# Seven-product spreading with sums left in PSUM, and a planner that picks each operation's engine first

## The chip, the cores and the metric

The kernel runs on one NeuronCore of a Trainium2 chip. The metric is the time on the device in microseconds; the time before is the median of three runs. The profile is of one further execution, whose span is 1522.8 us at a granted TensorE clock of 0.999.

The engines are named as in the profile: PE is TensorE's matmuls, PEld its weight loads, DVE is VectorE, ACT is ScalarE, POOL is GpSimd (called Pool here), SP issues the transfers.

## What is computed

64 graphs of 256 nodes with 128 features (`x`, 64 x 256 x 128, float32) pass through four layers that share one 256 x 256 adjacency matrix. Each layer is a residual with a layer norm: `x = norm(x + layer(x))`. The first layer is the one that the change touches most:

```python
def step(h, _):                       # 5 times
    m_in = jnp.einsum('nm,bmd->bnd', in_matrix, h)     # in_matrix = out_matrix = adj
    m_out = jnp.einsum('nm,bmd->bnd', out_matrix, h)
    av = jnp.concatenate([m_in, m_out], axis=-1)
    u3 = h @ u3_w.T + u3_b
    z = jax.nn.sigmoid(av @ w3_w.T + w3_b + u3)
    r = jax.nn.sigmoid(av @ w4_w.T + w4_b + u3)
    hv = jnp.tanh(av @ w5_w.T + w5_b + (r * h @ u5_w.T + u5_b))
    return (1.0 - z) * h + z * hv
```

The second layer mixes two linear maps of the nodes by a softmax of the edges, the third is an attention over the neighbours followed by a small perceptron, the fourth sums seven weighted propagations up to `adj^3`.

## The kernel before

**Tiles.** Two graphs make a pair; there are 32 pairs. A pair's state is one tile of 128 partitions x 512 columns, four blocks of 128 x 128: two graphs by two halves of the nodes.

**Layer 0.** In each of five steps the state `h` (nodes on partitions) is multiplied by the adjacency matrix ("spread", giving `mT` with features on partitions), and the gates follow: products L679, L680, L687, L694 and L695 of 512 columns, three tanh on ACT (L683, L689, L697), four elementwise operations on DVE (L685, L699, L700, L702). The new state is transposed by `turn` (L520 to L528), either by a DVE block transpose and two transfers over HBM, or by four TensorE transposes (L514). `BY_DMA` says for each place how many of the last pairs use TensorE.

**Spreading.** `spread` (L539) makes the two graphs' 256 x 256 product from four matmuls of 256 columns. `spread7` (L562) makes the same from seven matmuls of 128 columns (the Strassen-Winograd scheme). Four small sums of blocks of `h` come first, L573 to L576 (recorded at L558), on DVE or Pool. The products land in the four 128-column parts of one PSUM bank: X, Y, Z, V. Two of the parts are used again for a later product after they have been read. The results are put together outside PSUM by two copies (L569 on ACT, L570 on DVE) and four additions `plus` on DVE (L566): three of 128 columns and one of 256. `FIRST` and `FINAL` say how many pairs at either end use the plain spread: none at the start, the last three.

**The planner.** Nothing runs in the order of the text. Each operation is recorded in `Schedule.add` with its possible engines and a time for each, and `Schedule.order` is a list scheduler: in each turn it takes, of all operations whose inputs are ready and for which a tile is free, the one with the least key. Its result is the fixed order of every engine's queue; on the chip the engines run their queues in that order and wait for each other by semaphores. What the planner assumes:

- A dependent operation on another engine sees a result `LAG` plus a part by engine (`SEEN`) after its end. All times but TensorE's are multiplied by `MARGIN`.
- `USES`: a DVE operation with two SBUF inputs (DVE+) and every Pool operation hold a common resource PORT, so that the plan never has two of them at once.
- Where an operation may run on several engines, every way is a candidate of its own, and its key is its end (with `SPARE` of the engine); an operation with one way has its start as the key. After that comes how late the pair is against its due time (`DUE`, `LAST_DUE` for the `LAST` last pairs, `HOLD` by layer).
- `CLASSES` is the number of tiles of each kind. PS are the eight PSUM banks.

In `stats` and `scale_stats` each normalization has two small Pool operations: adding epsilon (L604, L648, L650) and a power of -0.5 (L607, L651), both on 128 x 4.

Of the kernel before, what the change touches and what calls it, by code (L numbers as in the profile page):

```python
# [9 lines left out]
ALU = mybir.AluOpType  # L10
AX = mybir.AxisListType

P = 128
N = 256
D = 128
STEPS = 5

BY_DMA = {"h": 0, "y": 2, "x1": 3, "x2": 2, "w": 3, "z": 1, "x3": 2}

WARM = 4  # L20


FAST = (0, 1, 2, 3, 4)
FIRST, FINAL = 0, 3

TURN, TT = 0.44, 0.61
LN_EPS = 1e-5
# [9 lines left out]
ROWS = ["l1_bias", "bp", "b1", "gat_g", "gat_b", "b2"]  # L37


CLASSES = {"X": (512, 15), "T": (512, 3), "A": (512, 34), "H": (520, 4), "B": (1024, 6), "S": (32, 64), "PS": (512, 8), "D": (512, 4), "E": (1024, 8)}  # L40

SEEN = {"PE": 0.23, "ACT": 0.16, "DVE": 0.16, "POOL": 0.12, "SP": 0.0}

USES = {"DVE+": ("DVE", "PORT"), "POOL": ("POOL", "PORT")}

AGAIN = {"DVE": 0.12, "POOL": 0.12}

SPARE = {"DVE": 0.0, "DVE+": 0.0, "POOL": 0.0}


DUE, LAST_DUE, LAST = 20.0, 9.0, 8

MARGIN, LAG = 1.03, 0.8

HOLD = (0.0, -20.0, 0.0, 80.0)


def mm(cols):
# [35 lines left out]
class Op:  # L94
    def __init__(self, pair, ways, reads, writes, number, dma):
        self.pair, self.ways, self.reads, self.writes, self.number, self.dma = pair, ways, reads, writes, number, dma
        self.seen = LAG + (sum(dma) if dma else SEEN[ways[0][0].rstrip("+")])
        self.before, self.then, self.waits, self.ready, self.rest = {}, [], 0, 0.0, 0.0


class Schedule:
# [29 lines left out]
    def order(self, tiles):  # L131
        for op in self.ops:
            op.waits = len(op.before)
            for b in op.before:
                b.then.append(op)
            for v in op.holds:
                v.left += 1
        for op in reversed(self.ops):
            us = min(w[1] for w in op.ways) + op.seen
            op.rest = us + max((x.rest for x in op.then if x.pair == op.pair), default=0.0)  # L140
        free = {cls: [(0.0, t) for t in ts] for cls, ts in tiles.items()}
        full = {}
        engines = dict.fromkeys([*SEEN, "PORT"], 0.0)
        ready = [op for op in self.ops if not op.waits]
        out, moved = [], 0.0
        while ready:
            best = None
            for op in ready:
                held = 0.0
                for v in op.holds:  # L150
                    if v.cls and v.ap is None:
                        held = max(held, min((t for t, a in free[v.cls] if full.get(id(a)) or not v.seeded), default=1e9))
                if held == 1e9:
                    continue
                for engine, us, fn in op.ways:
                    us = us if engine == "PE" else us * MARGIN
                    start = max(op.ready, held, *(engines[e] for e in USES.get(engine, (engine,))))
                    late = self.due(op.pair) - op.rest + HOLD[op.layer] if op.pair >= 0 else -1e4
                    key = (start + (us + SPARE.get(engine, 0.0) if len(op.ways) > 1 else 0.0), late, op.number)
                    if best is None or key < best[0]:  # L160
                        best = key, start, op, engine, us, fn
            if best is None:
                raise RuntimeError("no operation can start: too few tiles")
            _, start, op, engine, us, fn = best
            ready.remove(op)
            for v in op.holds:
                if v.cls and v.ap is None:
                    slot = min((s for s in free[v.cls] if full.get(id(s[1])) or not v.seeded), key=lambda s: s[0])
                    free[v.cls].remove(slot)
                    v.ap = slot[1]  # L170
            end = start + us
            engines.update(dict.fromkeys(USES.get(engine, (engine,)), end))
            if op.dma:
                wait, move, seen = op.dma
                moved = max(moved, end + wait) + move * MARGIN
                op.seen = moved + seen - end + LAG
            out.append((start, op.number, op, fn))
            for v in op.holds:
                v.left -= 1
                v.end = max(v.end, end + op.seen)  # L180
                if not v.left and v.cls:
                    free[v.cls].append((v.end, v.ap))
                    full[id(v.ap)] = v.full or v.seeded
            for x in op.then:
                x.waits -= 1
                same = engine != "SP" and x.ways[0][0].rstrip("+") == engine.rstrip("+")
                x.ready = max(x.ready, end + (AGAIN.get(engine.rstrip("+"), 0.0) if same else op.seen))
                if not x.waits:
                    ready.append(x)

            op.tiles = {v: v.ap for v in op.holds}
        assert len(out) == len(self.ops), "operations that wait for one another"
        self.span = max(engines.values())
        return [(op, fn) for _, _, op, fn in sorted(out, key=lambda x: x[:2])]
# [3 lines left out]
def kernel(ctx: ExitStack, tc: tile.TileContext, x, xT, adj, adjT, mats, cols, rows, out):  # L198
# [17 lines left out]
    def dve(us, fn, r, w):  # L216
        S.add([("DVE", us, fn)], r, w)
# [2 lines left out]
        S.add([("DVE+", us, fn)], r, w)  # L220

    def pool(us, fn, r, w):
        S.add([("POOL", us, fn)], r, w)

    def dve_or_pool(fn, r, w):

# [234 lines left out]

    aTt = fixed([4, P], "aTt")
    blk_a = lambda j, i: aT.ap[:, j, i * P:(i + 1) * P]
    for k, (p_, q_) in enumerate(((lambda: blk_a(0, 1), lambda: blk_a(0, 0)), (lambda: blk_a(1, 1), lambda: aTt.ap[:, 0, :]),
                                  (lambda: blk_a(1, 1), lambda: blk_a(0, 1)), (lambda: blk_a(1, 0), lambda: aTt.ap[:, 1, :]))):
        dve(0.25, lambda k=k, p_=p_, q_=q_: nc.vector.tensor_sub(aTt.ap[:, k, :], p_(), q_()), [aT, aTt], [aTt])
    centre(vx, lambda: vx.ap, 2)
    centre(vq, lambda: vq.ap, 2)

# [74 lines left out]
    def spread7(h, right, terms):  # L544


        sv, t, o = Value("A", name="sums"), bank(), Value("A", name="mT")
        p1, p2, p3, p4 = (Part(sv) for _ in range(4))
        X, Y, Z, V = (Part(t) for _ in range(4))
        o1, o2, o3 = (Part(o) for _ in range(3))  # L550
        blk = lambda v, k, n=1: v.at(512)[:, k * P:(k + n) * P]
        H = lambda b, j: lambda: blk(h, 2 * b + j)
        B = lambda j, i: lambda: right.ap[:, j, i * P:(i + 1) * P]
        T = lambda k: lambda: terms.ap[:, k, :]
        s1, s2, s3, s4 = (lambda k=k: blk(sv, k) for k in range(4))

        def add(o, x, y, op, r, w):
            fn = lambda e: e.tensor_tensor(o(), x(), y(), op=op)  # L558
            S.add([("DVE+", 0.2, lambda: fn(nc.vector)), ("POOL", 0.42, lambda: fn(nc.gpsimd))], r, w)

        def product(k, left, rt, r, w, start=False):
            pe(mm(128), lambda: nc.tensor.matmul(blk(t, k), left(), rt(), start=start, stop=True, skip_group_check=True),  # L562
               [*r, right, terms], w)

        def plus(to, k, other, r, w, n=1):
            dve(0.065 + 0.135 * n, lambda: nc.vector.tensor_add(to(), t.at(4, P)[:, k:k + n, :], other()), r, w)  # L566

        def copy(to, k, r, w):
            S.add([("ACT", 0.18, lambda: nc.scalar.copy(to(), blk(t, k))),  # L569
                   ("DVE", 0.2, lambda: nc.vector.tensor_copy(to(), blk(t, k)))], r, w)  # L570
        product(0, H(0, 0), B(0, 0), [h], [X, Y, Z, V], start=True)
        copy(lambda: blk(o, 3), 0, [X], [o3])
        add(s1, H(1, 0), H(1, 1), ALU.add, [h], [p1])  # L573
        add(s2, s1, H(0, 0), ALU.subtract, [h, p1], [p2])
        add(s3, H(0, 0), H(1, 0), ALU.subtract, [h], [p3])
        add(s4, H(0, 1), s2, ALU.subtract, [h, p2], [p4])  # L576
        product(0, H(0, 1), B(1, 0), [h, X], [X])
        copy(lambda: blk(o, 0), 0, [X], [o])
        product(1, s2, T(1), [p2, Y], [Y])
        plus(lambda: blk(sv, 1), 1, lambda: blk(o, 3), [Y, o3], [p2])  # L580
        product(2, s1, T(0), [p1, V], [V])
        product(3, s3, T(2), [p3, Z], [Z])
        plus(lambda: blk(sv, 0), 2, lambda: blk(sv, 1), [V, p2], [p1])
        product(2, s4, B(1, 1), [p4, V], [V])
        plus(lambda: blk(o, 3), 3, lambda: blk(sv, 0), [Z, p1, o3], [o])
        product(3, H(1, 1), T(3), [h, Z], [Z])
        plus(lambda: o.at(4, P)[:, 1:3, :], 2, lambda: blk(sv, 1)[:, None, :].to_broadcast([P, 2, P]), [V, Z, p2], [o], 2)
        return o

    def stats(y, eps=None):  # L590
# [306 lines left out]
```

## Time and profile before

| | |
|---|---|
| time, median of 3 runs | 1525.11 us (1524.67 to 1527.51) |
| span of the profiled execution | 1522.8 us |
| L562: products of seven, 2030 matmul records | 128 columns each |
| L539: plain spreads | 888 records of 256 columns |
| L679, L680, L687, L694, L695: gates | 320 records each, 512 columns |
| L566: additions out of PSUM | 435 of 128 columns, 145 of 256 |
| L569 and L570: copies out of PSUM | 265 on ACT, 25 on DVE |
| small sums of spread7 (L558) | 271 on DVE, 309 on Pool |
| L651 and L607: power on Pool, 128 x 4 | 192, median 1.04 us |

A float32 matmul stands in the records as two matmul instructions and two weight loads. In a line of the profile come the line of the kernel, engine, operation, `out<-in` by the program's names, the shapes and the count, then the busy time and the mean of one in nanoseconds; the idle time of that engine ahead of such instructions follows with what ended it. In a line of waits stand who waited, after `<-` for whom, the sum in us, the number of times and the longest. In a timeline line stand the start and the length in us, and in square brackets the idle time before it.

### The profile page before, as it was taken

How to read it: one execution, taken by the hardware profiler on the slowest of the kernel's cores; microseconds unless marked ns; L12 is line 12 of the kernel's file. 1: busy time of each engine (PE TensorE's matmuls, PEld its weight loads, DVE VectorE, ACT ScalarE, POOL GpSimd, SP SyncE). 2: the span in 40 equal slices, each digit the busy share in tenths (PEclk: the TensorE clock that was granted, in tenths of full speed). 3: DMA queues.
4: the chain of work that ended last, by engine and by line, in shares of the span. 5: the costliest groups of instructions: out<-in, count | busy, mean ns of one | idle time of the engine just before them, and what ended most of it. 6: DMA issues, size and time to landing. Idle time of an engine off the chain costs nothing.

```text
span 1522.8 us, 26241 instructions
## 1 busy us (share of the span) xinstructions
PE 1502.2 (99%) x7190; PEld 1063.2 (70%) x7190; DVE 1296.3 (85%) x3443; ACT 936.2 (61%) x2805; POOL 562.4 (37%) x784
## 2 busy tenths in 40 slices
PE   9999999999999999999999999999999999999998
PEld 6565656666666677677666776766767666788997
DVE  8988888888989898888998888899888788889763
ACT  2444445666776666656757567677657566768763
POOL 4322223243435433433443344334434132245542
PEclk9999999999999999999999999999999999999999
DMA  7544456576868788686696796767975877776441
GB/s 220 113 97 82 93 117 125 125 159 122 170 132 164 155 169 171 136 164 137 140 177 128 162 185 138 152 134 173 167 147 128 169 133 153 149 149 139 106 89 49
DMA packets 933874, 213.86 MB, mean 140 GB/s; under 512 B 715616, under 2 KB 929248, under 8 KB 933728
## 3 DMA queue, kind: packets, MB, share of 16 engines
q1 hardware_dynamic: 933728, 212.19, 68.6%
q8 instruction: 58, 0.95, 0.3%
q14 instruction: 88, 0.72, 0.2%
HBM read 115.55 MB, written 96.53 MB: 139 GB/s over the span
## 4 chain that ended last, share of the span: by engine, by line
PE 90%; DVE 6%; issue 1%; SPq 1%; DMA 1%; ACT 0%; POOL 0%; POOLq 0%; DVEq 0%; ACTq 0%
PE ps L562 14%; PE ps L539 12%; PE ps L694 8%; PE ps L695 8%; PE ps L687 8%; PE ps L679 8%; PE ps L680 8%; PE ps L716 7%; PE ps L786 4%; PE ps L830 3%; PE ps L822 3%; PE ps L823 3%; PE ps L746 2%; DVE a L566 1%; SPq L528 1%
## 5 line engine op out<-in xcount | busy, mean ns | idle before, releaser
L566 DVE TENSOR_TENSOR a<-ps,a 128x128 f32<-128x128 f32 (+1 forms) x580 | 174.5, 313 | 89.8 <-PE ps L562 75.4
L562 PEld LDWEIGHTS ps<-aTt,a 128*128 128x128 f32 x1102 | 160.9, 192 | 60.1 <-issue 42.4
L683 ACT ACTIVATE a<-ps,bzrh 128x512 f32<-128x512 f32 x160 | 109.8, 686 | 138.3 <-PE ps L680 118.2
L697 ACT ACTIVATE a<-ps,bzrh 128x512 f32<-128x512 f32 x160 | 109.9, 687 | 130.3 <-PE ps L695 126.4
L562 PE MATMUL ps<-aTt,a 128*128 128x128 f32 x1102 | 180.0, 278 | 4.8 <-ACT a L569 3.7
L558 POOL TENSOR_TENSOR a<-a 128x128 f32<-128x128 f32 x138 | 81.8, 606 | 236.2 <-DMA a<-e 112.1
L694 PE MATMUL ps<-a,w 128*128 128x512 f32 x320 | 163.8, 594 | 0.2 <-DVE h L748 0.2
L695 PE MATMUL ps<-a,u5h 128*128 128x512 f32 x320 | 163.5, 592 | 0.2 <-DVE a L685 0.2
L680 PE MATMUL ps<-a,w 128*128 128x512 f32 x320 | 163.4, 592 | 0.0
L687 PE MATMUL ps<-a,w 128*128 128x512 f32 x320 | 162.5, 593 | 0.0
L520 DVE STREAM_TRANSPOSE a<-a 128x512 f32<-128x512 f32 x218 | 152.0, 700 | 3.1 <-ACT a L662 0.4
L562 PEld LDWEIGHTS ps<-aT,a 128*128 128x128 f32 x754 | 118.2, 191 | 52.1 <-issue 34.9
L689 ACT ACTIVATE a<-ps,bzrh 128x512 f32<-128x512 f32 x160 | 109.7, 687 | 68.1 <-PE ps L687 61.5
L716 PEld LDWEIGHTS ps<-W,a 128*128 128x128 f32 x1024 | 131.0, 192 | 26.1 <-issue 22.2
L569 ACT COPY a<-ps 128x128 f32<-128x128 f32 x265 | 66.3, 266 | 129.7 <-PE ps L562 81.1
L562 PE MATMUL ps<-aT,a 128*128 128x128 f32 x754 | 136.7, 278 | 5.5 <-DVE a L566 3.4
L651 POOL TENSOR_TENSOR s<-s,neg_half 128x4 f32<-128x4 f32 x128 | 136.9, 1070 | 9.9
L716 PE MATMUL ps<-W,a 128*128 128x128 f32 x1024 | 136.5, 275 | 0.1
L679 PE MATMUL ps<-a,W 128*128 128x512 f32 x256 | 130.9, 593 | 0.0
L231 ACT COPY a<-ps 128x512 f32<-128x512 f32 (+1 forms) x162 | 82.6, 513 | 73.8 <-PE ps L539 36.7
L643 ACT ACTIVATE a<-ps 128x128 f32<-128x128 f32 x428 | 112.5, 282 | 23.1 <-PE ps L716 8.6
L648 POOL TENSOR_SCALAR s<-s 128x4 f32<-128x4 f32 x96 | 29.0, 302 | 249.2 <-ACT a L643 218.9
(197 smaller groups left out, 3302.2 us busy)
## 6 DMA issues: line engine op xcount, KB each, us to landing
e<-a SPq DMA_DIRECT2D x278, 256.0 KB
a<-e SPq DMA_DIRECT2D x1112, 64.0 KB
e<-b SPq DMA_DIRECT2D x29, 512.0 KB
b<-e SPq DMA_DIRECT2D x116, 128.0 KB
x<-x_in SPq DMA_DIRECT2D x32, 256.0 KB
t<-xT_in SPq DMA_DIRECT2D x32, 256.0 KB
a<-d SPq DMA_DIRECT2D x32, 256.0 KB
y_out<-a SPq DMA_DIRECT2D x32, 256.0 KB
```

Of the source, the lines that this page charges most:

```text
L520: dve(n / 512 * 0.55 + 0.09, lambda: nc.vector.transpose(st.at(n), i.at(n)), [i], [st])
L539: nc.tensor.matmul(t.at(2, N)[:, b, :], tokens(i)[:, 2 * b + j, :], right.ap[:, j, :], start=(b == j == 0), stop=(j == 1), skip_group_chec ...
L562: pe(mm(128), lambda: nc.tensor.matmul(blk(t, k), left(), rt(), start=start, stop=True, skip_group_check=True), [*r, right, terms], w)
L566: dve(0.065 + 0.135 * n, lambda: nc.vector.tensor_add(to(), t.at(4, P)[:, k:k + n, :], other()), r, w)
L643: nc.scalar.activation(tokens(junk)[:, c, :], v.at(len(tiles), D)[:, k, :], AF.Square, scale=D ** -0.5, accum_out=mv()[:, c, 1:2])
L651: pool(1.02, lambda: nc.gpsimd.tensor_tensor(rs(), rs(), neg_half.ap, op=ALU.pow), [s, neg_half], [s])
L679: nc.tensor.matmul(t.at(512), mat("u3"), hT.at(512), start=True, stop=False)
L680: nc.tensor.matmul(t.at(512), w4.ap, mT.at(512), start=False, stop=True)
L687: pe(mm(512), lambda t=t, mT=mT: nc.tensor.matmul(t.at(512), w3.ap, mT.at(512), start=False, stop=True, skip_group_check=True), [w3, mT, t ...
L694: nc.tensor.matmul(t.at(512), w5.ap, mT.at(512), start=True, stop=False)
L695: nc.tensor.matmul(t.at(512), u5h.ap, r.at(512), start=False, stop=True)
L716: nc.tensor.matmul(tokens(t)[:, c, :], tokens(i)[:, c, :], w(), start=(first and k == c == 0), stop=(k == len(lefts) - 1), skip_group_chec ...
```

## The change

It does three things, and sets the planner's constants anew.

1. `spread7` uses a Winograd form in which the sums need PSUM as the accumulator: four products in turn are added onto part X, which is read after each; two onto V; one stands in Y. Copies (now four, on ACT or DVE) take X and V into the result's blocks, and three additions of 128 columns on DVE add further parts. Two of the four small sums become one operation of 256 columns. The terms of the adjacency matrix (`aTt`) change sign to match.
2. Pool's operations with one way (`pool`, the small operations of the normalizations) become POOL-, which takes the Pool engine but not PORT.
3. `Schedule.order` first chooses each operation's engine by its end with `SPARE`, and then compares operations by the start on that engine.

```diff
-BY_DMA = {"h": 0, "y": 2, "x1": 3, "x2": 2, "w": 3, "z": 1, "x3": 2}
+BY_DMA = {"h": 1, "y": 0, "x1": 3, "x2": 3, "w": 0, "z": 4, "x3": 0}
-FIRST, FINAL = 0, 3
+FIRST, FINAL = 2, 0
-CLASSES = {"X": (512, 15), "T": (512, 3), "A": (512, 34), "H": (520, 4), "B": (1024, 6), ...}
+CLASSES = {"X": (512, 15), "T": (512, 4), "A": (512, 30), "H": (520, 6), "B": (1024, 5), ...}
-USES = {"DVE+": ("DVE", "PORT"), "POOL": ("POOL", "PORT")}
+USES = {"DVE+": ("DVE", "PORT"), "POOL": ("POOL", "PORT"), "POOL-": ("POOL",)}
-SPARE = {"DVE": 0.0, "DVE+": 0.0, "POOL": 0.0}
+SPARE = {"DVE": 0.6, "DVE+": 0.0, "POOL": -0.3}
-DUE, LAST_DUE, LAST = 20.0, 9.0, 8
+DUE, LAST_DUE, LAST = 15.0, 12.0, 12
-MARGIN, LAG = 1.03, 0.8
+MARGIN, LAG = 1.1, 0.3
-HOLD = (0.0, -20.0, 0.0, 80.0)
+HOLD = (0.0, -20.0, 0.0, 40.0)
...
+                way = None
                 for engine, us, fn in op.ways:
                     us = us if engine == "PE" else us * MARGIN
                     start = max(op.ready, held, *(engines[e] for e in USES.get(engine, (engine,))))
-                    late = self.due(op.pair) - op.rest + HOLD[op.layer] if op.pair >= 0 else -1e4
-                    key = (start + (us + SPARE.get(engine, 0.0) if len(op.ways) > 1 else 0.0), late, op.number)
-                    if best is None or key < best[0]:
-                        best = key, start, op, engine, us, fn
+                    end = start + us + SPARE.get(engine, 0.0)
+                    if way is None or end < way[0]:
+                        way = end, start, op, engine, us, fn
+                late = self.due(op.pair) - op.rest + HOLD[op.layer] if op.pair >= 0 else -1e4
+                key = (way[1], late, op.number)
+                if best is None or key < best[0]:
+                    best = key, *way[1:]
...
     def pool(us, fn, r, w):
-        S.add([("POOL", us, fn)], r, w)
+        S.add([("POOL-", us, fn)], r, w)
...
-        product(0, H(0, 0), B(0, 0), [h], [X, Y, Z, V], start=True)
-        copy(lambda: blk(o, 3), 0, [X], [o3])
-        add(s1, H(1, 0), H(1, 1), ALU.add, [h], [p1])
-        add(s2, s1, H(0, 0), ALU.subtract, [h, p1], [p2])
-        add(s3, H(0, 0), H(1, 0), ALU.subtract, [h], [p3])
-        add(s4, H(0, 1), s2, ALU.subtract, [h, p2], [p4])
-        product(0, H(0, 1), B(1, 0), [h, X], [X])
-        copy(lambda: blk(o, 0), 0, [X], [o])
-        product(1, s2, T(1), [p2, Y], [Y])
-        plus(lambda: blk(sv, 1), 1, lambda: blk(o, 3), [Y, o3], [p2])
-        product(2, s1, T(0), [p1, V], [V])
-        product(3, s3, T(2), [p3, Z], [Z])
-        plus(lambda: blk(sv, 0), 2, lambda: blk(sv, 1), [V, p2], [p1])
-        product(2, s4, B(1, 1), [p4, V], [V])
-        plus(lambda: blk(o, 3), 3, lambda: blk(sv, 0), [Z, p1, o3], [o])
-        product(3, H(1, 1), T(3), [h, Z], [Z])
-        plus(lambda: o.at(4, P)[:, 1:3, :], 2, lambda: blk(sv, 1)[:, None, :].to_broadcast([P, 2, P]), [V, Z, p2], [o], 2)
+        product(0, H(0, 0), B(0, 0), [h], [X, Y, V], start=True)
+        sum_(0.335, 0.8, lambda e: e.tensor_sub(sv.at(4, P)[:, 0:2], h.at(4, P)[:, 0::2], h.at(4, P)[:, 2:4]), [h], [p1])
+        sum_(0.2, 0.46, lambda e: e.tensor_sub(s2(), s1(), H(0, 0)()), [h, p1], [p2])
+        sum_(0.2, 0.46, lambda e: e.tensor_add(s4(), s2(), H(0, 1)()), [h, p2], [p4])
+        copy(0, 0, [X], [o0])
+        product(1, s1, T(0), [p1, V], [V])
+        copy(3, 1, [V], [o3])
+        product(2, H(0, 1), B(1, 0), [h, Y], [Y])
+        plus(0, 2, [Y, o0], [o, o0])
+        product(0, s2, T(1), [p2, X], [X])
+        copy(1, 0, [X], [o1])
+        product(1, s4, B(1, 1), [p4, V], [V])
+        plus(1, 1, [V, o1], [o, o1])
+        product(0, s3, T(2), [p1, X], [X])
+        plus(3, 0, [X, o3], [o, o3])
+        product(0, H(1, 1), T(3), [h, X], [X])
+        copy(2, 0, [X], [o])
```

More of the change, by code (lines that the diff above doesn't have):

```diff
@@ L37 @@
 ROWS = ["l1_bias", "bp", "b1", "gat_g", "gat_b", "b2"]
-CLASSES = {"X": (512, 15), "T": (512, 3), "A": (512, 34), "H": (520, 4), "B": (1024, 6), "S": (32, 64), "PS": (512, 8), "D": (512, 4), "E": (1024, 8)}
+CLASSES = {"X": (512, 15), "T": (512, 4), "A": (512, 30), "H": (520, 6), "B": (1024, 5), "S": (32, 64), "PS": (512, 8), "D": (512, 4), "E": (1024, 8)}
 SEEN = {"PE": 0.23, "ACT": 0.16, "DVE": 0.16, "POOL": 0.12, "SP": 0.0}
-USES = {"DVE+": ("DVE", "PORT"), "POOL": ("POOL", "PORT")}
+USES = {"DVE+": ("DVE", "PORT"), "POOL": ("POOL", "PORT"), "POOL-": ("POOL",)}
 AGAIN = {"DVE": 0.12, "POOL": 0.12}
-SPARE = {"DVE": 0.0, "DVE+": 0.0, "POOL": 0.0}
-DUE, LAST_DUE, LAST = 20.0, 9.0, 8
-MARGIN, LAG = 1.03, 0.8
-HOLD = (0.0, -20.0, 0.0, 80.0)
+SPARE = {"DVE": 0.6, "DVE+": 0.0, "POOL": -0.3}
+DUE, LAST_DUE, LAST = 15.0, 12.0, 12
+MARGIN, LAG = 1.1, 0.3
+HOLD = (0.0, -20.0, 0.0, 40.0)
 def mm(cols):
@@ L96, in __init__ @@
         self.pair, self.ways, self.reads, self.writes, self.number, self.dma = pair, ways, reads, writes, number, dma
-        self.seen = LAG + (sum(dma) if dma else SEEN[ways[0][0].rstrip("+")])
+        self.seen = LAG + (sum(dma) if dma else SEEN[ways[0][0].rstrip("+-")])
         self.before, self.then, self.waits, self.ready, self.rest = {}, [], 0, 0.0, 0.0
@@ L185, in order @@
                 x.waits -= 1
-                same = engine != "SP" and x.ways[0][0].rstrip("+") == engine.rstrip("+")
-                x.ready = max(x.ready, end + (AGAIN.get(engine.rstrip("+"), 0.0) if same else op.seen))
+                same = engine != "SP" and x.ways[0][0].rstrip("+-") == engine.rstrip("+-")
+                x.ready = max(x.ready, end + (AGAIN.get(engine.rstrip("+-"), 0.0) if same else op.seen))
                 if not x.waits:
@@ L463 @@
     blk_a = lambda j, i: aT.ap[:, j, i * P:(i + 1) * P]
-    for k, (p_, q_) in enumerate(((lambda: blk_a(0, 1), lambda: blk_a(0, 0)), (lambda: blk_a(1, 1), lambda: aTt.ap[:, 0, :]),
-                                  (lambda: blk_a(1, 1), lambda: blk_a(0, 1)), (lambda: blk_a(1, 0), lambda: aTt.ap[:, 1, :]))):
-        dve(0.25, lambda k=k, p_=p_, q_=q_: nc.vector.tensor_sub(aTt.ap[:, k, :], p_(), q_()), [aT, aTt], [aTt])
+    dve(0.25, lambda: nc.vector.tensor_sub(aTt.ap[:, 0, :], blk_a(0, 1), blk_a(0, 0)), [aT], [aTt])
+    for k, other in ((1, lambda: aTt.ap[:, 0, :]), (2, lambda: blk_a(0, 1))):
+        dve(0.25, lambda k=k, other=other: nc.vector.scalar_tensor_tensor(aTt.ap[:, k, :], blk_a(1, 1), -1.0, other(),
+                                                                         op0=ALU.mult, op1=ALU.subtract), [aT, aTt], [aTt])
+    dve(0.25, lambda: nc.vector.tensor_add(aTt.ap[:, 3, :], aTt.ap[:, 1, :], blk_a(1, 0)), [aT, aTt], [aTt])
     centre(vx, lambda: vx.ap, 2)
@@ L544, in spread7 @@
     def spread7(h, right, terms):
[L547 to L550, printed above, removed]
+        sv, t, o = Value("A", name="sums"), Value("PS", name="ps"), Value("A", name="mT")
+        p1, p2, p4 = (Part(sv) for _ in range(3))
+        X, Y, V = (Part(t) for _ in range(3))
+        o0, o1, o3 = (Part(o) for _ in range(3))
         blk = lambda v, k, n=1: v.at(512)[:, k * P:(k + n) * P]
@@ L554, in spread7 @@
         T = lambda k: lambda: terms.ap[:, k, :]
[L555 to L559, printed above, removed]
+        s3, s1, s2, s4 = (lambda k=k: blk(sv, k) for k in range(4))
         def product(k, left, rt, r, w, start=False):
@@ L563, in product, with sum_ @@
                [*r, right, terms], w)
-        def plus(to, k, other, r, w, n=1):
-            dve(0.065 + 0.135 * n, lambda: nc.vector.tensor_add(to(), t.at(4, P)[:, k:k + n, :], other()), r, w)
+        def sum_(us, us_pool, fn, r, w):
+            S.add([("DVE+", us, lambda: fn(nc.vector)), ("POOL", us_pool, lambda: fn(nc.gpsimd))], r, w)
         def copy(to, k, r, w):
-            S.add([("ACT", 0.18, lambda: nc.scalar.copy(to(), blk(t, k))),
-                   ("DVE", 0.2, lambda: nc.vector.tensor_copy(to(), blk(t, k)))], r, w)
@@ L581, in spread7 @@
-        product(2, s1, T(0), [p1, V], [V])
-        product(3, s3, T(2), [p3, Z], [Z])
-        plus(lambda: blk(sv, 0), 2, lambda: blk(sv, 1), [V, p2], [p1])
-        product(2, s4, B(1, 1), [p4, V], [V])
-        plus(lambda: blk(o, 3), 3, lambda: blk(sv, 0), [Z, p1, o3], [o])
-        product(3, H(1, 1), T(3), [h, Z], [Z])
-        plus(lambda: o.at(4, P)[:, 1:3, :], 2, lambda: blk(sv, 1)[:, None, :].to_broadcast([P, 2, P]), [V, Z, p2], [o], 2)
+            S.add([("ACT", 0.18, lambda: nc.scalar.copy(blk(o, to), blk(t, k))),
+                   ("DVE", 0.2, lambda: nc.vector.tensor_copy(blk(o, to), blk(t, k)))], r, w)
@@ new lines, in plus @@
+        def plus(to, k, r, w):
+            dve(0.2, lambda: nc.vector.tensor_add(blk(o, to), blk(t, k), blk(o, to)), r, w)
+        product(0, H(0, 0), B(0, 0), [h], [X, Y, V], start=True)
[3 more added lines that the diff above has]
+        copy(0, 0, [X], [o0])
```

## The prediction

> **What bounds the kernel now.** I read the page's engine totals first, then the stretches (busy time of each engine by window), then who waited for whom on TensorE, then the chain of waits, and last the timeline around single TensorE waits. Page, part 1:
>
> ```profile
> span 1522.8 us, 26241 instructions
> PE 1502.2 (99%) x7190; PEld 1063.2 (70%) x7190; DVE 1296.3 (85%) x3443; ACT 936.2 (61%) x2805; POOL 562.4 (37%) x784
> ```
>
> TensorE is idle for only 1522.8 - 1502.2 = 20.6 us, so the kernel can win no more than idle time, the last few microseconds, and columns that it no longer streams. Where the idle time lies (columns: window, its length, then busy us of PE, PEld, DVE, ACT, POOL):
>
> ```profile
> 0.00:25.00 25.00, 22.08 (x90) 15.52 (x91) 20.56 (x68) 6.18 (x14) 11.09 (x27) 1.00 0.98 281
> 25.00:50.00 25.00, 24.25 (x127) 16.24 (x126) 24.96 (x67) 9.62 (x23) 15.41 (x25) 1.00 0.42 95
> 50.00:200.00 150.00, 150.00 (x599) 87.57 (x598) 126.17 (x296) 62.52 (x126) 33.01 (x56) 1.00 0.47 99
> 200.00:600.00 400.00, 394.15 (x1877) 267.63 (x1876) 353.57 (x930) 254.90 (x753) 152.27 (x211) 1.00 0.74 146
> 600.00:1100.00 500.00, 495.46 (x2443) 353.03 (x2443) 444.36 (x1178) 331.29 (x1036) 200.04 (x263) 1.00 0.77 154
> 1100.00:1500.00 400.00, 399.64 (x1984) 309.27 (x1983) 320.20 (x877) 265.49 (x842) 146.82 (x199) 1.00 0.66 133
> 1500.00:1523.00 23.00, 16.60 (x80) 13.97 (x78) 6.48 (x31) 6.17 (x17) 3.78 (x6) 0.92 0.16 46
> ```
>
> Idle: 3.7 us in the first 50, none to 200, 10.4 us from 200 to 1100 (there VectorE is 88 to 89% busy), 0.4 us to 1500, and 6.4 us at the end, after the last product. Who ended TensorE's waits between 50 and 1500 us:
>
> ```profile
> PE ps L562 <- DVE a L566: 4.4, 11, 1.1
> PE ps L562 <- ACT a L569: 3.3, 9, 0.5
> PE ps L786 <- ACT a L697: 0.7, 1, 0.7
> PE ps L562 <- DVE a L570: 0.6, 2, 0.4
> ```
>
> Nearly all stand before a product of spread7 (L562), waiting for an addition (L566) or copy (L569, L570) out of its own PSUM bank. A matmul's end is modelled, and hides part of a wait: summing each matmul's start-to-start distance beyond the median of its form, I get 26.8 us lost, 6.1 of it in the first 50 us and 20.7 later. The timeline shows what makes an addition late:
>
> ```profile
> 730.29 1.45 POOL L733 TENSOR_TENSOR a<-x,rbc 128x512 f32<-128x512 f32 x1
> 730.54 1.48 DVE L761 CUSTOM_DVE_ANT_0 b<-a,maskb 128x256 f32<-128x256 f32 x1
> 731.70 1.44 POOL L777 TENSOR_TENSOR b<-b,a 128x512 f32<-128x512 f32 x1
> 731.95 1.47 DVE L761 CUSTOM_DVE_ANT_0 b<-a,maskb 128x256 f32<-128x256 f32 x1
> 733.36 1.49 DVE L566 TENSOR_TENSOR a<-ps,a 128x128 f32<-128x128 f32 x6
> 734.80 0.46 PE L562 MATMUL ps<-aT,a 128*128 128x128 f32 x2 [0.84 <-DVE a L566]
> ```
>
> L761's median is 0.417 us; twice in a row it takes about 1.5 while Pool works on a large tile, six additions pile up behind it, and TensorE waits. Over the trace 163 VectorE instructions are more than 60 ns over the median of their form, 65 us in all, each beside a Pool operation of 128 columns or more.
>
> [...] Here one record of 512 columns starts 429 ns before the next, 256 takes 216 and 128 takes 112[...]; a product is two records. [...] the 71 VectorE instructions that ran beside the small power operations alone (L648, L651) together lost 0.03 us[...]. [...] Here 128 columns take 0.201 us start to start, 256 take 0.334. [...]
>
> **The change, part by part.** Counts are those of the two built programs, their instructions standing in the order that the planner gives.
>
> *TensorE's columns.* A plain spread is eight records of 256 columns, 8 x 0.216 = 1.73 us; the seven products are 14 x 0.112 = 1.57. FIRST 2 and FINAL 0 make 150 spreads of seven in place of 145: 5 x 0.16 = -0.8 us. BY_DMA leaves 56 transposes on TensorE in place of 64, each 0.109: -0.9. Together -1.7 us, and that is certain.
>
> *VectorE.* Before, 145 double additions (0.334) and 435 single ones (0.201) emptied the bank: 48.4 + 87.4 = 135.8 us. After, 450 single ones: 90.5. The four small sums before each spread become one of double width and two single: on VectorE 271 x 0.202 = 54.7 becomes 86 x 0.334 + 42 x 0.202 = 37.2. Copies out of the bank go 25 to 32, +1.4. Against it the choice of engines moves 144 pieces of the layer norm from ScalarE to VectorE (L615, 0.338 long, about 0.26 apart): +37. Fewer evacuations, scalings and statistics on VectorE give -30, more multiplications and additions of constants +11. Sum: about -43 us of 1296, so 82% in place of 85%.
>
> *ScalarE.* Copies 265 to 568 at 0.161: +49; the layer norm's pieces 232 to 88 at 0.385: -55; scaling, evacuation and squares +20. About +14, 62%. It has room.
>
> *Pool.* 309 single sums at 0.458 become 64 double and 258 single: with the planner's 0.8 for the double (none is in the trace) about 169 us against 142; eight large operations fewer, -10. [...] the collisions stay.
>
> *The round trips.* This is the part that can go either way. In the new spread7 one PSUM quarter is used four times: product, copy, product, copy, product, addition, product, copy. The shortest round trip product, copy, product in the trace is some 0.52 us, with an addition 0.55. I counted the TensorE work that stands, in each program's order, between a product and the next one that needs its quarter emptied. Before, the median is 5.2 us for the copied quarter, one trip in ten below 2.4. After, the medians of the four trips are 2.4 to 3.1 us, one in ten below 1.5 to 1.8, none below 0.88. The planner's LAG of 0.3 in place of 0.8 does that. So at one trip in ten the cushion is about 1 us, and a single collision costs the same: a lone one mostly fits, two in a row don't. In return only one of the four trips goes through VectorE. Before, the sixth product waited for two chained additions and the seventh for a third, each in VectorE's queue behind L761 or L699. MARGIN 1.1 (1.03 before) plans VectorE, ScalarE and Pool slower than they are, which gives back cushion at every queue. Leaving the small power operations off the port removes 192 x (1.02 + 0.23) = 240 us of holding[...].
>
> *Start.* Before, the first products wait for sums, copies and additions on a VectorE that also builds the constants: about 2.2 us in two gaps at 8.7 and 11.9 us. After, pairs 0 and 1 use plain spreads, which need the input alone, and the gate products of pair 0 follow after the second spread, behind which the evacuation of the first hides: -2 us. [...]
>
> *End.* The last product, statistics, power, scaling and output stay a chain of 6 us; two squares on ScalarE in place of VectorE's statistics are worth -0.2 at most. I count 0.
>
> *BY_DMA, DUE, LAST, HOLD, CLASSES.* They reorder pairs. Transfers ended a single TensorE wait of 0.4 us (L746); I cost them at nothing, with the DMA's lag in the range.
>
> Sum: -1.7 columns, -2 start, and of the 20.7 us lost in the middle I take half, because two of the three VectorE steps that release products are gone while the cushion halves: -10. 1525.1 - 13.7 = about 1511.5 us.
>
> **The rivals.**
> *Nearly all waits go.* For it: after 1100 us TensorE already runs 399.64 of 400 with VectorE at 80%, and VectorE now falls by 3 points. Against: the late stretch has few spreads of seven (148 of 2030 records). Losing all but 3 us of the middle gives 1525.1 - 1.7 - 2 - 17.7 = about 1503.7.
> *No change.* The shorter distances lose as much again as the lighter VectorE saves, and 10 to 14 us come back: 1523. For it: the waits today come although distances are twice as long.
> *Slower.* VectorE is late by 65 / 163 = 0.4 us on average at 163 instructions; the changed program has about 400 round trips closer than 2.2 us where before had 29. If 60 of those meet a collision and lose 0.25 us each, +15 on top of today's, with the -3.7 that is safe: about 1536. Against: three of the four trips go through ScalarE[...].
>
> **How the numbers follow.** Forecast 0.50, nearly all waits go 0.18, no change 0.12, slower 0.20. Faster is the first two: 0.68. The range runs from 1502 (all waits gone and a little off the end) to 1533, above which I leave half of the slower case.
>
> **What would show it.** Right: TensorE busy 99.5% with its idle time before 1500 us at 7 or less; VectorE near 1253 us; first gap at 8.7 us gone. Wrong: more waits of products for copies on ScalarE (the cushion was too small), waits for DMA at the sums, or VectorE not falling since collisions grow with the double sums on Pool.

## The result and the profile after

The changed kernel took 1516.24 us (median of 4 runs, 1516.03 to 1516.94) against 1525.13 us (1524.67 to 1527.51) before, a ratio of 0.9939 with an interval of [0.9922, 0.9957]. The span of the profiled execution went from 1522.8 to 1514.4 us. The engine totals on the page of the kernel after:

```profile
span 1514.4 us, 26315 instructions
PE 1499.2 (99%) x7212; PEld 1059.6 (70%) x7212; DVE 1219.7 (81%) x3240; ACT 960.5 (63%) x3056; POOL 587.0 (39%) x789
```

VectorE lost 76.6 us of work, ScalarE gained 24.3, Pool 24.6, and TensorE is idle for 15.2 us where it was 20.6. The same stretches as before the change (window, its length, busy us of PE, PEld, DVE, ACT, POOL):

```profile
0.00:25.00 25.00, 23.29 (x91) 16.36 (x92) 14.26 (x46) 8.36 (x18) 6.01 (x13) 1.00 1.02 291
25.00:50.00 25.00, 25.00 (x97) 15.02 (x97) 23.75 (x55) 12.13 (x28) 17.12 (x27) 1.00 0.49 117
50.00:200.00 150.00, 148.42 (x575) 88.20 (x574) 110.46 (x236) 70.01 (x163) 31.30 (x48) 1.00 0.47 97
200.00:600.00 400.00, 396.93 (x1903) 269.02 (x1902) 343.80 (x886) 266.81 (x828) 160.28 (x207) 1.00 0.76 153
600.00:1100.00 500.00, 497.88 (x2428) 353.34 (x2427) 410.44 (x1102) 320.26 (x1038) 203.01 (x270) 1.00 0.73 149
1100.00:1500.00 400.00, 399.25 (x2089) 310.97 (x2088) 316.13 (x919) 277.84 (x961) 166.72 (x220) 1.00 0.68 135
1500.00:1514.50 14.50, 8.38 (x38) 6.72 (x36) 0.85 (x2) 5.08 (x23) 2.52 (x4) 0.92 0.24 61
```

The first 50 us lose 1.7 us of TensorE in place of 3.7, and 200 to 1100 us lose 5.2 in place of 10.4; but 50 to 200 us, which lost nothing, now lose 1.6. Who ended TensorE's waits between 50 and 1500 us, after the change:

```profile
PE ps L565 <- DVE a L576: 4.1, 10, 0.5
PE ps L565 <- ACT a L572: 1.8, 5, 0.4
```

Both the products that waited for additions (L566 before, L576 now) and those that waited for copies on ScalarE (L569 before, L572 now) did so for less time; no DMA is left among them. Measured as in the prediction (start-to-start distances of matmuls beyond the median of their form), TensorE lost:

| us lost | first 50 | 50 to 1500 | after 1500 | sum |
|---|---|---|---|---|
| before | 6.0 | 20.5 | 0.3 | 26.8 |
| after | 2.25 | 17.7 | 0.3 | 20.2 |

So the 8.4 us of the spans are 3.8 from the start, 2.8 from the middle, and 1.8 from columns that are no longer streamed and the rounding of the rest. The middle, for which most was expected, gave the least for its size.

### The profile page after: what moved, and what is told of

Read it like the earlier page. It is cut to its first block, busy times and chain, and to the rows that moved or that the text cites. A ratio compares the mean times of both kernels' runs of the same rounds, so it can differ in the third digit from the quotient of the medians.

```text
span 1514.4 us, 26315 instructions
## 1 busy us (share of the span) xinstructions
PE 1499.2 (99%) x7212; PEld 1059.6 (70%) x7212; DVE 1219.7 (81%) x3240; ACT 960.5 (63%) x3056; POOL 587.0 (39%) x789
## 4 chain that ended last, share of the span: by engine, by line
PE 96%; DVE 1%; DMA 1%; ACT 1%; issue 0%; POOL 0%; SPq 0%; POOLq 0%; ACTq 0%; DVEq 0%
PE ps L565 16%; PE ps L545 12%; PE ps L701 9%; PE ps L702 9%; PE ps L686 9%; PE ps L687 9%; PE ps L694 9%; PE ps L723 7%; PE ps L793 4%; PE ps L829 3%; PE ps L830 3%; PE ps L837 3%; PE ps L753 2%; DMA x<-x_in 1%; PE ps L520 0%
## 5 line engine op out<-in xcount | busy, mean ns | idle before, releaser
L565 PEld LDWEIGHTS ps<-aTt,a 128*128 128x128 f32 x1140 | 180.9, 191 | 99.2 <-issue 65.8
L576 DVE TENSOR_TENSOR a<-ps,a 128x128 f32<-128x128 f32 x450 | 117.1, 283 | 118.2 <-PE ps L565 84.5
L565 PE MATMUL ps<-aTt,a 128*128 128x128 f32 x1140 | 204.6, 277 | 2.9 <-DVE a L576 1.7
L572 ACT COPY a<-ps 128x128 f32<-128x128 f32 x568 | 137.3, 269 | 109.6 <-PE ps L565 90.3
L235 ACT COPY a<-ps 128x512 f32<-128x512 f32 (+1 forms) x178 | 91.5, 517 | 106.7 <-PE ps L830 57.1
L580 POOL TENSOR_TENSOR a<-a,a 128x128 f32<-128x128 f32 x101 | 61.9, 613 | 230.9 <-DVE a L579 142.1
L650 ACT ACTIVATE a<-ps 128x128 f32<-128x128 f32 x452 | 119.6, 281 | 47.2 <-PE ps L723 20.8
L723 PE MATMUL ps<-W,a 128*128 128x128 f32 x1024 | 147.2, 275 | 0.0
L658 POOL TENSOR_TENSOR s<-s,neg_half 128x4 f32<-128x4 f32 x128 | 141.6, 1106 | 9.8
L707 DVE SCALAR_TENSOR_TENSOR a<-a,a 128x512 f32<-128x512 f32 x160 | 117.4, 735 | 4.9 <-ACT a L696 3.9
```

Of the source, the lines that this page charges most:

```text
L572: S.add([("ACT", 0.18, lambda: nc.scalar.copy(blk(o, to), blk(t, k))), ("DVE", 0.2, lambda: nc.vector.tensor_copy(blk(o, to), blk(t, k)))] ...
L650: nc.scalar.activation(tokens(junk)[:, c, :], v.at(len(tiles), D)[:, k, :], AF.Square, scale=D ** -0.5, accum_out=mv()[:, c, 1:2])
L658: pool(1.02, lambda: nc.gpsimd.tensor_tensor(rs(), rs(), neg_half.ap, op=ALU.pow), [s, neg_half], [s])
L723: nc.tensor.matmul(tokens(t)[:, c, :], tokens(i)[:, c, :], w(), start=(first and k == c == 0), stop=(k == len(lefts) - 1), skip_group_chec ...
```

## The experiments

Each kernel was timed beside the kernel before on the same chip, whose medians there were 1524.04 to 1524.35 us, where it was 1525.13 us beside the changed kernel. A difference to the changed kernel's 1516.24 us is therefore uncertain by about 1 us. "Changed" and "before" in the table name the kernel from which a run starts. The times, with where TensorE lost what in the one profiled execution (us):

| run | time, us | ratio to before | lost: first 50 | 50 to 1500 | after 1500 |
|---|---|---|---|---|---|
| e1, changed, old form | 1523.80 | 0.9996 [0.9988, 1.0004] | 3.1 | 23.7 | 0.3 |
| e2, changed, PORT held again | 1518.34 | 0.9960 [0.9945, 0.9975] | 1.2 | 16.6 | 2.7 |
| e3, changed, old key | 1555.12 | 1.0202 [1.0187, 1.0217] | 2.2 | 51.1 | 3.5 |
| e5, changed, LAG 0.8 | 1548.86 | 1.0162 [1.0145, 1.0180] | 1.2 | 38.5 | 18.8 |
| e7, before, new form | 1548.02 | 1.0156 [1.0137, 1.0175] | 7.5 | 26.7 | 20.4 |
| e8, before, FIRST 2 | 1531.05 | 1.0053 [1.0040, 1.0067] | 1.75 | 28.5 | 0.3 |
| e10, before, LAG 0.3 | 1544.88 | 1.0136 [1.0121, 1.0151] | 4.9 | 37.5 | 5.8 |
| e11, before, new form, LAG 0.3 | 1535.51 | 1.0075 [1.0058, 1.0092] | 5.8 | 30.7 | 0.3 |
| e16, before, engine first | 1552.14 | 1.0185 [1.0168, 1.0201] | 5.7 | 22.2 | 27.7 |
| e17, changed, MARGIN 1.09 | 1520.89 | 0.9980 [0.9971, 0.9989] | 3.0 | 21.3 | 0.3 |
| e18, changed, old key, SPARE 0 | 1559.32 | 1.0228 [1.0202, 1.0253] | 3.5 | 60.3 | 1.9 |
| e19, changed, other constants | 1511.60 | 0.9921 [0.9907, 0.9936] | 1.75 | 14.1 | 0.3 |

**One part undone: the form.** The new planner and constants, with spread7 and aTt of before:

```diff
-        sv, t, o = Value("A", name="sums"), Value("PS", name="ps"), Value("A", name="mT")
+        sv, t, o = Value("A", name="sums"), bank(), Value("A", name="mT")
...
-        copy(2, 0, [X], [o])
+        plus(lambda: o.at(4, P)[:, 1:3, :], 2, lambda: blk(sv, 1)[:, None, :].to_broadcast([P, 2, P]), [V, Z, p2], [o], 2)
```

> The changed kernel with the seven-product form of before (Z as a fourth part, additions outside PSUM); everything else as changed. Theory A, the form: three chained VectorE additions ahead of the sixth and seventh product come back, so TensorE's waits in the middle grow from some 18 to 25 us or more and the time rises to 1521 or above. Theory B, the planner: the form only moves work between VectorE and ScalarE, the gain is the order that the new constants give; the time stays within 2 us of 1516. In both the start (first 50 us) stays near 2 us lost.

It took 1523.8 us, as long as the kernel before: next to the other parts, the form is worth 7.6 us. The time is what theory A said; the loss in the middle, 23.7 us, stayed a little under its 25. The first line of the edit has a side effect that was not separated: `bank()` marks the tile as written in full, and the planner lets other operations seed only such a tile. The three largest rows of who ended TensorE's waits from 50 to 1500 us in this kernel:

```profile
PE ps L566 <- DVE a L570: 5.6, 17, 0.5
PE ps L566 <- ACT a L573: 2.9, 9, 0.5
PE ps L566 <- POOL a L562: 2.0, 6, 0.4
```

All three rows are longer or new against the changed kernel's two, so the loss is in the same place, the products of seven (L566 here).

**One part undone: the port.** POOL- holds PORT again, as all of Pool did before.

```diff
-USES = {"DVE+": ("DVE", "PORT"), "POOL": ("POOL", "PORT"), "POOL-": ("POOL",)}
+USES = {"DVE+": ("DVE", "PORT"), "POOL": ("POOL", "PORT"), "POOL-": ("POOL", "PORT")}
```

> The changed kernel with Pool's small operations holding PORT in the plan again, all else as changed. The trace shows no VectorE delay beside the power operation, so the plan keeps VectorE off for up to 240 us that the chip doesn't need. If that matters: TensorE's lost time in the middle grows from 18 to 23 us or more, time 1521 or above. If VectorE has room enough at 81%: within 2.5 us of 1516.

1518.34 us, 2.1 more than the changed kernel. The profiled execution was the fastest of four, 1516.42 us, and lost 20.4 us in all against 20.2. This part moves little or nothing.

**One part undone: the choice of engine.** Every way is a candidate again.

```diff
-                    end = start + us + SPARE.get(engine, 0.0)
-                    if way is None or end < way[0]:
-                        way = end, start, op, engine, us, fn
...
+                    key = (start + (us + SPARE.get(engine, 0.0) if len(op.ways) > 1 else 0.0), late, op.number)
+                    if best is None or key < best[0]:
+                        best = key, start, op, engine, us, fn
```

> The changed kernel with the key of before: an operation with several engines is compared by its end with SPARE, one with a single engine by its start. Operations with a choice (the sums that release products, the copies) come later by their own length plus 0.6. Theory: that lengthens the chain of three copies and an addition in every spread, so the time rises by 3 us or more (1519 or above). Rival: a shift by under a microsecond is lost in the order, within 2.5 us of 1516.

1555.12 us, 39 more, where the theory had asked for 3 or more. The first four rows of who ended TensorE's waits in this kernel, 50 to 1500 us:

```profile
PE ps L561 <- DVE a L572: 5.4, 12, 1.2
PE ps L561 <- ACT a L568: 4.4, 7, 1.3
PE ps L561 <- DMA a<-e: 2.7, 3, 1.3
PE ps L789 <- DMA b<-e: 2.4, 2, 1.3
```

Waits for DMA, which the changed kernel does not have, are among the largest. The run has a flaw: in the old key SPARE counts as time, so that 0.6 on VectorE also delays an operation against others. A later run takes that out:

```diff
-SPARE = {"DVE": 0.6, "DVE+": 0.0, "POOL": -0.3}
+SPARE = {"DVE": 0.0, "DVE+": 0.0, "POOL": 0.0}
```

> The changed kernel with the planner's key of before (operations ranked by the end that they would have) and SPARE all 0, so that SPARE does not enter the key as a penalty on VectorE's operations. Theory S (the run with the old key and SPARE 0.6 lost 39 us to that penalty): 1530 us or less. Rival K (the key itself costs it: short operations overtake long ones, as with the old key and LAG 0.3 in the kernel before, 1545 us): 1540 us or more.

1559.32 us: it is not the penalty. The old key is slow with these constants, with the penalty and without it. Why it delays what TensorE waits for was not followed further.

**One part undone: the small LAG.** The changed kernel with LAG as before.

```diff
-MARGIN, LAG = 1.1, 0.3
+MARGIN, LAG = 1.1, 0.8
```

> The changed kernel with LAG 0.8 in place of 0.3. One round trip in ten of spread7 stands then at 3.0 us or less, not at 2.0. Theory C, the cushion: the short distances are why the middle lost 18 us and not 10; with more distance it loses 10 to 13 and the time is 1509 to 1512. Theory D, lateness elsewhere: waits come from queues that stand behind something else; more distance keeps pairs and banks longer, the time is 1516 or above.

1548.86 us. A plan with more cushion is 33 us slower, and 18.8 us of its loss come after 1500 us, in single waits of up to 4.0 us, like those shown below for the choice of engine alone. Theory C, that short distances cost the middle its gain, is out: with more distance the middle lost 38.5 us, not 10 to 13.

**Single parts in the kernel before.** The form alone:

> The kernel before with the new seven-product form alone, all constants and the planner's choice as before. Theory A, the form: VectorE's busy time falls by 30 us or more, the waits in the middle go from 21 to about 14 us, time about 1518. Theory B, the planner: no gain without the constants, 1524 to 1527. The start stays as before (6 us lost in the first 50).

1548.02 us, slower by 24, of which 20 again in the tail. Neither forecast had that. Plain spreads for the first two pairs alone (`FIRST` 0 to 2):

> The kernel before with FIRST 2 in place of 0: pairs 0 and 1 use plain spreads. Ten plain spreads more cost 10 x 0.16 = 1.6 us of columns. If the plain start is what wins the first 50 us (6.0 us lost before, 2.2 after), 3 to 4 us come back there and the time is about 1523; if the start was won by the other order, the time is 1526 to 1527.

Its first 50 us lose 1.75 in place of 6.0, so the change's gain at the start is that of the plain spreads, 4 us. The middle of this other order loses 8 us more than before, and the run is slower as a whole, outside both forecasts. The small LAG alone (0.8 to 0.3):

> The kernel before with LAG 0.3 alone. Theory E, chain length in the plan: the old form has one copied trip and a chain of two additions, so a shorter lag shortens a step there too, but less; time 1519 to 1525. Theory F, the cushion of my prediction: the old form has VectorE additions in both late trips and loses with shorter distances: 1527 or above.

1544.88 us: 17 us more in the middle. The losses over 150 ns at products of seven between 50 and 1500 us grew from 13.8 to 26.5 us. Form and small LAG together:

> The kernel before with the new form and LAG 0.3, all other constants and the planner as before. Theory E: the lag was what made the new form slow with the old constants (1548 us); the last pair's layer 0 now ends at 1366 us of TensorE's work, not at 1401, and the 20 us lost at the end go: time 1518 to 1526. Rival: the loss came from the other constants (PORT, DUE, MARGIN): 1535 or above.

1535.51 us (1534.65 to 1535.76), at the edge of the rival's 1535 and far from theory E's 1518 to 1526. Theory E had the tail right: that of e7 is gone (0.3 in place of 20.4). The middle stays bad (30.7). Engine first alone, with the form and all constants of before:

```diff
-                    key = (start + (us + SPARE.get(engine, 0.0) if len(op.ways) > 1 else 0.0), late, op.number)
-                    if best is None or key < best[0]:
-                        best = key, start, op, engine, us, fn
+                    end = start + us + SPARE.get(engine, 0.0)
+                    if way is None or end < way[0]:
+                        way = end, start, op, engine, us, fn
```

> The kernel before with one edit: the planner picks each operation's engine first, by its earliest end, and then ranks operations by their start. Seven-product form, all constants, FIRST 0 as before. Theory G (the choice of engine is a gain of its own, whatever form and constants): 1515 to 1521 us, ratio 0.994 to 0.998, idle TensorE between matmuls after 50 us below 17 us. Rival H (the choice pays only beside the small LAG; with LAG 0.8, as in the run of the changed kernel with LAG 0.8, it gains nothing): 1525 us or more.

1552.14 us. The middle is as before (22.2 against 20.5) but the end is empty. Rows of TensorE in the timeline of this run near its end:

```profile
1505.18 2.05 PE L790 MATMUL ps<-h,b 128*128 128x128 f32 x16 [0.24 <-ACT b L235]
1512.49 3.78 PE L543 MATMUL ps<-ginT,a 128*128 128x256 f32 x8 [5.26 <-DVE a L799]
1517.44 2.07 PE L720 MATMUL ps<-W,a 128*128 128x128 f32 x8 [1.17 <-ACT ps L235]
1523.19 1.11 PE L518 MATMUL ps<-ident,a 128*128 128x128 f32 x4 [3.68 <-DVE a L668]
1526.31 2.08 PE L720 MATMUL ps<-W,a 128*128 128x128 f32 x8 [2.00 <-ACT ps L235]
```

From the second on, each short block of matmuls waits 1 to 5 us for the elementwise work after the block before: no product of another pair fills the wait.

**A change with no mechanism.** The changed kernel with the planner's costs 1% lower.

```diff
-MARGIN, LAG = 1.1, 0.3
+MARGIN, LAG = 1.09, 0.3
```

> The changed kernel with MARGIN 1.09 in place of 1.10: the costs that the planner works with are 1% lower, and no mechanism of the change is touched. It measures what an accidental other order is worth. Theory N (the constants sit on a lucky order, and any other order costs as much as undoing a part does): 1523 us or more. Rival R (the order is robust, and the differences of the single-part runs are mechanism): 1514 to 1519 us.

1520.89 us, 4.7 more than the changed kernel, between the two forecasts. Set against the kernel before in the same session, it gains 3.2 us in place of 8.9. So half of the gain or more depends on which of several near orders the constants happen to give. It is one nudge alone, and others may move more or less. Differences of this size between single-part runs say nothing of a mechanism: the port's 2.1 us is inside it, the form's 7.6 not far outside.

**Other constants for the same code.**

```diff
-BY_DMA = {"h": 1, "y": 0, "x1": 3, "x2": 3, "w": 0, "z": 4, "x3": 0}
+BY_DMA = {"h": 1, "y": 0, "x1": 3, "x2": 3, "w": 0, "z": 0, "x3": 0}
-SPARE = {"DVE": 0.6, "DVE+": 0.0, "POOL": -0.3}
+SPARE = {"DVE": 0.6, "DVE+": -0.3, "POOL": -0.3}
-DUE, LAST_DUE, LAST = 15.0, 12.0, 12
+DUE, LAST_DUE, LAST = 14.3, 9.3, 12
-MARGIN, LAG = 1.1, 0.3
+MARGIN, LAG = 1.13, 0.23
```

> The changed kernel with other constants: BY_DMA z 0, SPARE DVE+ -0.3, DUE 14.3, LAST_DUE 9.3, MARGIN 1.13, LAG 0.23. Theory L (an order with still fewer waits of VectorE's and ScalarE's copies exists within the same form and key): 1511 to 1515 us, idle TensorE between matmuls 17 us or less. Rival M (the changed kernel's order is near what single constants give, and collisions decide the rest): 1517 us or more.

1511.60 us (1510.5 to 1514.08), below every run of the changed kernel, as theory L had it. Two stretches of it:

```profile
200.00:600.00 400.00, 400.00 (x1943) 274.62 (x1942) 358.92 (x945) 266.48 (x844) 151.97 (x187) 1.00 0.77 154
600.00:1100.00 500.00, 496.87 (x2408) 350.85 (x2407) 417.37 (x1162) 322.20 (x1074) 137.65 (x185) 1.00 0.74 149
```

TensorE is busy through 400 us on end, with VectorE busier than after the change (358.92 against 343.80), so VectorE's load alone doesn't make the waits there.

**What the products wait for.** No experiment was made for this; it is read from the traces and from the semaphores of the built programs. The products, copies, additions and sums of spread7 stand in a trace in the order of the plan, engine by engine, so each can be matched with its call in the program. Rows of the changed kernel's timeline, TensorE and ScalarE:

```profile
189.92 0.39 PE L565 MATMUL ps<-aTt,a 128*128 128x128 f32 x2
190.14 1.02 PE L694 MATMUL ps<-a,w 128*128 128x512 f32 x2
...
190.49 0.26 ACT L572 COPY a<-ps 128x128 f32<-128x128 f32 x1
...
191.00 0.38 PE L565 MATMUL ps<-aTt,a 128*128 128x128 f32 x2
...
191.48 0.27 ACT L572 COPY a<-ps 128x128 f32<-128x128 f32 x1 [0.74 <-PE ps L565]
...
191.80 0.49 PE L565 MATMUL ps<-aT,a 128*128 128x128 f32 x2 [0.41 <-ACT a L572]
```

The product at 189.92 writes part V of a bank. The copy at 191.48 reads V, which was complete at about 190.3, and ScalarE was free from 190.75 (the copy at 190.49 is another pair's); yet it waited until the product at 191.00 ended, which writes part X. The product at 191.80 writes part Y, which nobody had read, and it began 0.05 us after the end of the copy of V. In the plan X, Y and V are parts with histories of their own; in the program, engines take turns at the whole bank.

The same can be asked of every loss over 150 ns at a product of seven between 50 and 1490 us. In the kernel before, 26 of 29 (11.5 of 13.8 us) began within 0.18 us after the end of a read of another part of their bank that the plan doesn't let them wait for, while the copies, additions and sums that it does had ended earlier. After the change it is 30 of 32 (12.2 of 12.7 us), in e19 17 of 20 (7.9 of 9.8 us). In every one of these cases (26, 30 and 17), of the semaphores that the product waits for in the built program, the one that came last is that of the read of the other part; for the product at 191.80 it is the copy of V. So the program itself orders the two, and they don't merely fall together in time. Among products that lost less than 60 ns only 10 of 969 before and 18 of 1007 after follow such a read so closely. VectorE's lateness beside Pool can explain fewer: 12 of all 35 losses over 150 ns in the middle of the kernel before had VectorE instructions late by over 0.2 us together in the 3 us ahead, where a fifth of all moments have that; after the change 8 of 32, against 15%.

Why the program orders reads and writes of different parts of a bank is not shown by these runs. Nor was it tried to give the planner the same order, or to put X, Y and V into different banks, which would show what it is worth. Until then it is shown what TensorE waits for, and not what the time would be without it.

## Why the prediction was right or wrong

The prediction gave 1511.5 us, 1502 to 1533, and faster with 0.68. The time is in the range, 4.7 us above the number. How near it came says little: the middle gave 7 us less than forecast, the start about 2 more, and the nudge without a mechanism moves as much as the miss. Of the signs named for being right, the first gap went; TensorE was busy for 99.0% of the span, not 99.5, and idle for 9.2 us before 1500 us, not 7 or less.

- *Columns*, -1.7: the counts came out as built, 2100 records of the products of seven in place of 2030; the remainder of the spans agrees within their rounding.
- *Start*, -2: right mechanism, too small. It gave 3.8 us, and the run with the plain spreads alone shows the same 4. The gap at 8.7 us is gone, as foretold.
- *VectorE*, -43 to about 1253 us: it fell 76.6, to 1219.7. The kinds of work came out near the working: additions out of PSUM 153.6 to 106.0 us (-47.6, against -45.3 expected), pieces of the layer norm +39.6 (+37). Up to 20 of the 34 us more are lateness beside Pool: VectorE instructions over 60 ns beyond their form's median lost 65.2 us in all before and 45.3 after (163 and 117 of them, each beside a Pool operation of 128 columns or more), where I had left the collisions as they were.
- *ScalarE*, +14: +24.3; at 63% busy it has the room. *Pool*: the double sum takes 0.73 us at the median, the planner's 0.8 was near.
- *The middle*, "of the 20.7 us lost in the middle I take half ...: -10": this is the step that failed. It fell 2.8 us, from 20.5 to 17.7. I reasoned from one timeline, in which additions were late behind L761 and Pool, to all waits. And I counted "the TensorE work ... between a product and the next one that needs its quarter emptied". In the built program the products wait for reads of the bank's other parts too, at 26 of 29 of the losses over 150 ns before and 30 of 32 after. The losses over 150 ns at products of seven, the waits that the argument was about, only went from 13.8 to 12.7 us, and the waits for other parts of the bank among them even grew, from 11.5 to 12.2. Of these 30 waits after the change 19 were for additions on VectorE, although by quarters only one trip in four goes through VectorE. What else went were large losses at other products, 2.6 us before and none after. By quarters no trip in either plan has under 0.55 us of TensorE's work, the time of the shortest trip with an addition; by banks 30 have in the kernel before and 17 after, and under 0.88 us about 49 and 68. A lighter VectorE, on which the half rested, puts no more of TensorE's work into these trips, and there are more of the next shortest after the change.
- *The cushion.* That LAG 0.3 makes trips shorter was right, but that it only costs was not: with 0.8 the changed kernel needs 33 us more, 18.8 of them after 1500 us. In both kernels that joined LAG 0.8 to the new form (e5, e7), and in the one that joined it to the choice of engine (e16), the tail lost 19 to 28 us; with 0.3 and the new form (after, e11) it lost 0.3. The step that made BY_DMA, DUE and the rest free of cost had no place for such a tail.
- *End*, 0: right, 0.3 us lost in both. DMA: right in the changed kernel.
- *The rivals.* Slower, by round trips that are too close, fits what e10 shows of LAG 0.3 with the old form and key (+21 us). The changed kernel with the old key (e3, e18) is slow too, so the new key may be what keeps it from that; with waits for DMA among theirs, these runs don't isolate it. The "about 400 round trips closer than 2.2 us" can't be right: 150 spreads have 600 trips, and with medians of 2.4 to 3.1 us fewer than half of them are closer. Counted again in the built program they are 215, and by the rival's own rule its +15 becomes about +8. The port's release had been given no gain of its own, and e2 agrees.

What each of the three edits is worth by itself can't be added up. The form alone costs 24 us, LAG 0.3 alone 21, the choice of engine alone 28, and all together with the other constants gain 9. For the start the cause is shown (e8); for the middle, by how much each part moves it, the runs don't tell it from the order of the plan. Which of those constants closes the gap between e11 and the changed kernel beside the choice of engine stays open.

## What to carry to other kernels

Before counting round trips through PSUM, ask what the program really orders: here parts of a bank that the plan treats as independent are ordered as one, and the waits sit there (12.2 of the 12.7 us lost over 150 ns at products of seven after the change). Test a set of constants by a nudge with no mechanism too: here it moved 4.7 us where the gain was 8.9. And look at the tail of every run: where nothing is left to fill the last waits, TensorE stands empty at the end, whatever the middle won: 18.8 to 27.7 us were lost there in e5, e7 and e16.

## What was not expected of the hardware

- Single sums on Pool of 128 columns take 0.458 us at the median; one of 256 takes 0.73, hence less than two. The changed kernel's rows of the double sums, with shortest, median and longest in ns and the first and last start:

```profile
L579 DVE TENSOR_TENSOR a<-a x67: 375/418/1469, 47.3 to 1356.3; 128x256 f32<-128x256 f32 x67
L579 POOL TENSOR_TENSOR a<-a x53: 722/732/1267, 58.0 to 1305.0; 128x256 f32<-128x256 f32 x53
```

Both reach 1.3 to 1.5 us: either side takes longer at times, not VectorE alone. Of Pool's 64 double sums 22 took over 0.9 us. Of these 21 began while VectorE was in an instruction with two inputs from SBUF, and of the other 42 only 5 did.

- The granted TensorE clock was lower in stretches in which TensorE had little to do. The last stretch of the run with engine first alone, from 1500 us on (the first of the last three numbers is the clock):

```profile
1500.00:1552.00 52.00, 28.33 (x106) 21.66 (x104) 15.96 (x60) 8.99 (x23) 7.07 (x11) 0.67 0.05 15
```

It is 0.67 there, with TensorE busy for 28.33 us until the span ends at 1551.6, and 0.99 over the whole span; in the changed kernel's short last stretch it is 0.92. The timeline rows of this run above show what it does: 16 matmul records of 128 columns take 2.05 us at 1505, and 8 take 2.07 us at 1517, which is 0.26 us each in place of 0.13; in the page's last slice of the span, from 1512.8 us on, the clock is at 5 tenths. So this drained tail is paid for twice, by waiting and by slower matmuls. No run changes the load alone, so what sets the clock is not shown.
